# A four-layer block for four sequences: two elements' ternary layers cut in two, their rounded rows held in WKV's buffers

## The chip, the cores and the metric

The kernel runs on one core of a Trainium2 chip. A core has a matrix engine (TensorE, "PE" in the profile, with "PEld" for its weight loads), a vector engine (VectorE, "DVE"), a scalar engine (ScalarE, "ACT"), a general engine (GpSimd, "POOL") and SyncE ("SP"), whose queue issues the DMAs here. Each engine works through its own queue in order; semaphores tie the queues to each other. The metric is the device time of one execution in microseconds (us). Lower is better.

## What is computed

Four sequences ("elements", b = 0 to 3) of 512 rows and 512 columns go through four layers, each added to x with a gate:

```python
x = x + tanh(g_xattn[0]) * wkv(layernorm(x), context)
x = x + tanh(g_ffn[0])   * bit_ffn(layernorm(x))      # 512 -> 2048 -> 512, 1-bit weights
x = x + tanh(g_xattn[1]) * attention(layernorm(x), context)   # 16 heads, int8 rounding
x = x + tanh(g_ffn[1])   * ternary(layernorm(x), gamma, W)

def ternary(x, gamma, W):
    xn = x * rsqrt(mean(x * x) + 1e-6) * gamma
    a = 127 / (max(abs(xn), row) + 1e-5)
    x_q = clip(round(xn * a), -128, 127) / a
    w = 1 / (mean(abs(W)) + 1e-5)
    w_q = clip(round(W * w), -1, 1) / w
    return x_q @ w_q.T
```

`bit_ffn` rounds its input, and the product of its two halves, to int8 with one scale for each 64 columns, and its weights to their sign. The elements don't depend on each other. The change concerns the last layer, the ternary one.

## The kernel before

Rows are worked on in tiles of 128 (NT = 4 tiles an element), all in float32 or in pairs of halves, and each element's x stays on the chip (`xb`). The four elements form a pipeline. While the FFN of element b runs on PE, the attention of element b - 1 is threaded between its matmuls, and the WKV layer of element b + 1 as well. The FFN of an element takes 16 units (NT row tiles x NF = 4 column blocks, `ff_hp` and `ff_acc` in the profile); the attention takes 64 score blocks (`s_ps`, `at_nm`, `at_P`, `pt_ps`, `at_PT`, `o_ps`).

The order of this is written out by hand. Every layer is a generator that yields after each step; `line(gen, (start, end, steps), ...)` gives its steps places on an axis on which 1 is one element's FFN and 1/SLOTS (SLOTS = 17) is one unit; and `run` always advances the generator whose next step has the smallest place. PE's instructions come out in this order. On the other engines a scheduler orders them by when their inputs are expected; each engine's queue is then fixed. A line marked `aside` is put near the end of the unit in which its place lies.

On that axis the FFN of element b runs from b to b + 16/17. The attention of element b has its 72 unit steps from `start` = b + 1 + 4.95/17 to `end` = `start` + 18/17, so it reaches a little into the next element's FFN; the attention of the last element has no FFN beside it. The ternary layer of element b follows its attention, `late_by` behind `end`: 8 units later for b = 0, 9 for b = 1. So the ternary layer of b = 0 lies beside the fourth element's FFN's start (rounding and products within some 700 to 782 us of the trace) and that of b = 1 behind the last FFN (some 892 to 953 us). That of b = 2 lies beside the last element's attention (some 987 to 1022), and that of b = 3 ends the kernel.

A row tile of the ternary layer goes like this (`ternary`, lines 1130 to 1175). For b = 0 and 1, POOL centres and scales the rows (`centred_aside`, L219) and multiplies by gamma (L1148) into `tf_xn`; for b = 2 and 3, DVE does both in one instruction (L1141). DVE takes the largest absolute value (`absmax`, L222) and derives the factors in `tf_s` with small operations (L1152, L1153, L1159, L1160). ACT rounds (`rounded`, L231). Then come the products: four PE transposes into a bank `qr_ps` (L165, called in `transposed_rows`), an ACT copy that takes the rounding constant away (L238, `tf_xT`), four PE matmuls into `f_ps` (L162), DVE's addition to x (L1173), and the output's DMA on SP (L1174). `in_steps(chains, 1)` runs the four tiles one step apart.

Where the buffers lie: `tf_xn` of b = 0 comes from a ring of ROWS = 3 rows, `at_row`, which the attention's own rows `at_xn` use too; for b = 1 to 3 it comes from a ring of three in the FFN's pool. `tf_s` has a ring of four. `qr_ps`, `f_ps` and the attention's `pt_ps`, `ot_ps` and `o_ps` share the three PSUM banks with the tag `m`; the FFN's `ff_hp` and the attention's scores `s_ps` use the three with the tag `hp`. The WKV layer keeps its work in a pool of its own, among it `wk_k` and `wk_e`, each [128, 4, 512] float32, last used by the WKV of the last element.

Other names in the text: the FFN's quantiser takes group maxima (`qg_s`, L222, L676), rounds (`qg_i`, L680), casts on ACT into the single buffer `qg_b` (L684) and scales back on POOL (`ff_xn` or `ff_z`, L685); `ff_z` is formed by ACT L745, DVE L746 and L750; `tp_ps` are the FFN's transposes; L773 adds the FFN's result to x. In the attention, `at_nm` is the score maximum (DVE L948), `at_P` the exponential (ACT L950), `at_PT` the copy of the transposed weights (DVE L968 or ACT L970), L1000 and L1036 the scaling of results, and L1037 the addition to x on POOL. Its queries are rounded and projected (`at_xn`, `at_s`, `q_ps`, `at_half`), written to DRAM by the DMA `qD` and fetched again in the layout of the scores by `at_qR`, both on SP's queue. The layer norm takes its statistics on DVE (L191, L194, L200, L204) and its square root on POOL (L180, L207), giving `ln_r` and `ln_m`.

Of the kernel before, what the change touches and what calls it, by code (L numbers as in the profile page):

```python
# [10 lines left out]
F32 = mybir.dt.float32  # L11
F32R = mybir.dt.float32r
BF16 = mybir.dt.bfloat16
# [8 lines left out]
P = 128  # L22
# [8 lines left out]
def kernel(  # L31
# [37 lines left out]
    NB, T, D = x.shape  # L69
    FF = w1.shape[0]  # L70
    NT, NC, NF = T // P, D // P, FF // D
# [4 lines left out]
    ROWS = 3  # L76
# [4 lines left out]
    sm = ctx.enter_context(tc.tile_pool(name="small", bufs=4))  # L81
    ring = ctx.enter_context(tc.tile_pool(name="ring", bufs=5))
    ff = ctx.enter_context(tc.tile_pool(name="ffn", bufs=2))
    wk = ctx.enter_context(tc.tile_pool(name="wkv", bufs=1))
# [46 lines left out]
    def bank(name, dtype=F32):  # L131

        return psum_tile(name, "m", dtype)
# [22 lines left out]
    def next_turn():  # L156

        if "last" in turn:
            turn["ahead"] = turn["last"]

    def matmul(*args, **kwargs):
        return in_turn(nc.tensor.matmul(*args, **kwargs))  # L162
# [54 lines left out]
    def centred_aside(dst, xb, r, t):  # L217

        nc.gpsimd.tensor_scalar(dst, xb[:, t, :], r[t][0], r[t][1], ALU.mult, ALU.add)  # L219

    def absmax(dst, src):
        nc.vector.tensor_reduce(dst, src, AX.X, ALU.max, apply_absolute_value=True)  # L222
# [6 lines left out]
    def rounded(src, r):  # L229

        nc.scalar.activation(src, src, AF.Identity, bias=magic[:, 0:1], scale=r)  # L231

    def transposed_rows(dst, src):

        pt = bank("qr_ps")
        for c in range(NC):
            transpose(pt[:, c * P : (c + 1) * P], src[:, c * P : (c + 1) * P], ident)
        nc.scalar.activation(dst, blocks(pt), AF.Identity, bias=magic[:, 1:2])  # L238

    def in_steps(chains, delay):  # L240


        ahead = []
        for j, chain in enumerate(chains):
            lag = delay * j if isinstance(delay, int) else delay[j]
            ahead += [(k + lag, -j, chain) for k in range(10)]
        for _, group in groupby(sorted(ahead, key=lambda a: a[:2]), key=lambda a: a[0]):
            went = False
            for _, _, chain in group:
                went = next(chain, None) is not None or went  # L250
                next_turn()
            if went:
                yield
# [22 lines left out]
    class Weights:  # L276
# [130 lines left out]
        def ternary(self):  # L407
            wn = self.raw.pop("f")
            mf = self.mean_abs(self.fsum, D * D)
            nc.vector.tensor_scalar(mf, mf, 1e-5, None, ALU.add)  # L410
            nc.vector.tensor_scalar(
                coef[:, 3:4], mf, gates[:, 3:4], 1.0 / 127.0, ALU.mult, ALU.mult
            )
            rf = cp.tile([P, 1], F32, name="rf")
            nc.vector.reciprocal(rf, mf)
            wi = self.pool.tile([P, NC, D], BF16, name="wi", tag="sg", bufs=2)
            self.ints["f"] = wi
            yield
            for j in range(NC):
                rounded(wn[:, j, :], rf)  # L420
                nc.vector.tensor_scalar(
                    wn[:, j, :], wn[:, j, :], MAGIC + 1.0, MAGIC - 1.0, ALU.min, ALU.max
                )
                nc.scalar.activation(
                    wi[:, j, :], wn[:, j, :], AF.Identity, bias=magic[:, 1:2]
                )
                yield
# [412 lines left out]
    def attention_layer(b, xb, pool, tiles=range(NT)):  # L840
# [209 lines left out]
        def end(ts):  # L1050

            yield from together([project_out(t) for t in ts])
            means, scale = statistics(b, xb, ts)
            yield from together([ternary(b, xb, pool, t, means, scale) for t in ts])
# [57 lines left out]
    def statistics(b, xb, tiles):  # L1112
# [13 lines left out]
        at = {t: slice(i, i + 1) for i, t in enumerate(tiles)}  # L1126
        return {t: m[:, at[t]] for t in tiles}, {t: y[:, at[t]] for t in tiles}

    def ternary(b, xb, pool, t, r, scale=None):


        last = b > NB - 3
        behind_ffn = b > NB - 4
        if behind_ffn:

            xn = ff.tile([P, D], F32, name="tf_xn", tag="ff_a", bufs=3)
        else:
            xn = pool.tile([P, D], F32, name="tf_xn", tag="at_row", bufs=ROWS)
        s = sm.tile([P, 3], F32, name="tf_s", tag="tf_s")
        if last:  # L1140
            nc.vector.scalar_tensor_tensor(  # L1141
                xn, xb[:, t, :], r[t], gamma_b, ALU.add, ALU.mult
            )
            absmax(s[:, 0:1], xn)
            nc.vector.tensor_scalar(s[:, 0:1], s[:, 0:1], scale[t], 1e-5, ALU.mult, ALU.add)
        else:
            centred_aside(xn, xb, r, t)
            nc.gpsimd.tensor_tensor(xn, xn, gamma_b, ALU.mult)  # L1148
            yield True
            yield True  # L1150
            absmax(s[:, 0:1], xn)
            nc.vector.tensor_scalar(s[:, 0:1], s[:, 0:1], 1e-5, None, ALU.add)  # L1152
        nc.vector.reciprocal(s[:, 1:2], s[:, 0:1])  # L1153
        if last:
            nc.vector.tensor_scalar(
                s[:, 1:2], s[:, 1:2], scale[t], 127.0, ALU.mult, ALU.mult
            )
        else:
            nc.vector.tensor_scalar(s[:, 1:2], s[:, 1:2], 127.0, None, ALU.mult)  # L1159
        nc.vector.tensor_tensor(s[:, 2:3], s[:, 0:1], coef[:, 3:4], ALU.mult)  # L1160
        rounded(xn, s[:, 1:2])
        yield True
        if behind_ffn:
            xT = ring.tile([P, NC, P], BF16, name="tf_xT", tag="w")
        else:
            xT = pool.tile([P, NC, P], BF16, name="tf_xT", tag="at_oqT")
        transposed_rows(xT, xn)
        yield True
        fp = bank("f_ps")
        for c in range(NC):  # L1170
            matmul(fp, lhsT=xT[:, c, :], rhs=wfT[:, c, :], start=(c == 0), stop=(c == NC - 1))
        xt = xb[:, t, :]
        nc.vector.scalar_tensor_tensor(xt, fp, s[:, 2:3], xt, ALU.mult, ALU.add)  # L1173
        nc.sync.dma_start(out=out[b, t * P : (t + 1) * P, :], in_=xt)  # L1174
        yield True
# [17 lines left out]
    def late(make):  # L1193
        yield from make()

    def place(line):

        k = line["step"]
        for start, end, steps in line["parts"]:
            if k < steps:  # L1200
                at = start + (end - start) * k / steps

                return (math.floor(at * SLOTS) + 0.8) / SLOTS if line["aside"] else at
            k -= steps
        return end

    def run(until):
        while lines:
            now = min(lines, key=place)
            if place(now) > until:  # L1210
                return
            try:
                next(now["gen"])
                now["step"] += 1
                next_turn()
            except StopIteration:
                lines.remove(now)
# [3 lines left out]
    SLOTS = NT * NF + 1  # L1221

    def line(gen, *parts, aside=False):
        lines.append({"gen": gen, "parts": parts, "step": 0, "aside": aside})

    xs = {}
# [122 lines left out]
    for b in range(NB):  # L1349
        if b:  # L1350
            early = (0.99, 1.0, 4) if b == 1 else (b - 0.19, b - 0.1, 3), (b - 0.08, b, 1)
            line(
                late(lambda b=b: ffn_layer(xs[b])),
                *((early[0],) if b == 1 else early),
                (b, b + 16 / SLOTS, 64),
                (b + 16 / SLOTS, b + 17.75 / SLOTS, 7),
            )
        start = b + 1 + 4.95 / SLOTS
        end = start + 18 / SLOTS
        line(  # L1360
            late(lambda b=b: attention_layer(b, xs[b], at)),
            (b + 1.0 if b == 0 else b + 0.7, b + 1.03 if b == 0 else b + 0.9, 5),
            (b + 1 + 1.7 / SLOTS, b + 1 + 3.7 / SLOTS, 5),
            (b + 1 + 3.75 / SLOTS, b + 1 + 4.35 / SLOTS, 2),
            (start, end, 72),
            (end, end + 2.4 / SLOTS, 6)
            if b != NB - 2
            else (end - 0.15 / SLOTS, end + 4.65 / SLOTS, 6),
            (end + 2.4 / SLOTS, end + 3.4 / SLOTS, 4),
        )  # L1370
        if b < NB - 1:
            late_by = (8 / SLOTS, 9 / SLOTS, 0.0)[b]
            line(
                late(lambda b=b: ternary_layer(b, xs[b], at)),
                (end + 3 / SLOTS + late_by, end + 8 / SLOTS + late_by, 8)
                if b < NB - 2
                else (end + 4.85 / SLOTS, end + 11.85 / SLOTS, 7),
                aside=b < NB - 2,
            )
    run(NB + 9)  # L1380


# [43 lines left out]
```

## Time and profile before

| | us |
|---|---|
| median of 3 runs (lowest to highest) | 1079.84 (1078.74 to 1081.25) |
| the profiled execution, its whole time | 1080.4 |
| its span, from the first instruction to the last | 1078.6 |
| mean granted PE clock | 0.967 |

The profile page covers one execution. Its first part gives each engine's busy time and its share of the span; its second part cuts the span in 40 slices of 27 us and gives the busy share of each slice in tenths. A stretch view gives the same for windows of one's choice. A timeline row has the start in us, the duration (of the whole group where an instruction comes several times in a row, "x2"), the engine, the source line, the operation, out<-in, and in brackets the idle time of the engine just before it and the instruction that ended it. Ends of PE matmuls are modelled, and neighbouring ones overlap. Two other rows of the page, the engines behind PE, in tenths of a slice:

```profile
DVE  5976547747876799987669799977687858799876
POOL 3831114413423244632215526333121303200000
```

The vector engine is busiest, beside PE, from about 860 us on; POOL has next to nothing to do in the last 130 us.

The costliest waits of the whole run, engine by engine (in total, times, longest), are few and short on PE, and longer on the engines that serve it:

```profile
POOL ff_z L685 <- ACT qg_b L684: 287.2, 50, 12.6
ACT at_PT L970 <- PE pt_ps L165: 70.8, 99, 2.2
ACT at_P L950 <- DVE at_nm L948: 38.1, 57, 4.2
```

### The profile page before, as it was taken

What the parts mean: (1) busy time and instruction counts of PE and PEld (TensorE: products, weight loads), DVE (VectorE), ACT (ScalarE), POOL (GpSimd) and SP (SyncE); (2) the same over time, 40 slices, a digit from 0 to 9 for tenths busy, and PEclk for the clock granted to TensorE, in tenths of its full rate; (3) what the DMA queues carried; (4) which work ended last, traced back from release to release, by engine and by line L of the source; (5) the groups of instructions that cost most, each with busy time, mean ns of one, the idle gap of its engine ahead of it and who ended that gap; (6) DMA issues with size and microseconds to landing.
All of it is one profiled execution on the core that took longest, in us unless ns stands there. A gap on an engine that the chain in (4) does not pass through costs nothing.

```text
span 1078.6 us, 17948 instructions
## 1 busy us (share of the span) xinstructions
PE 935.4 (87%) x6353; PEld 675.0 (63%) x6380; DVE 836.0 (78%) x1610; ACT 724.6 (67%) x1480; POOL 321.6 (30%) x328
## 2 busy tenths in 40 slices
PE   3879998998888888889998798999999998888875
PEld 2335565565656666767776476777677777655652
DVE  5976547747876799987669799977687858799876
ACT  6656756476555677667778677777676767777763
POOL 3831114413423244632215526333121303200000
PEclk8889999999999999999999799999999999999998
DMA  8188945365445673744665528445665662254311
GB/s 292 39 257 323 322 172 214 115 225 187 156 137 149 235 242 120 256 133 138 235 196 195 176 92 261 138 165 182 229 232 179 209 218 61 87 158 121 111 39 40
DMA packets 85672, 189.67 MB, mean 176 GB/s; under 512 B 12240, under 2 KB 36816, under 8 KB 74576
## 3 DMA queue, kind: packets, MB, share of 16 engines
q1 hardware_dynamic: 85584, 188.53, 53.2%
q8 instruction: 51, 0.84, 0.3%
q14 instruction: 37, 0.30, 0.1%
HBM read 148.65 MB, written 39.85 MB: 175 GB/s over the span
## 4 chain that ended last, share of the span: by engine, by line
PE 45%; DVE 26%; ACT 13%; issue 5%; DMA 5%; POOL 5%; SPq 1%; ACTq 0%; POOLq 0%; DVEq 0%
PE ff_hp L162 14%; PE pt_ps L165 7%; PE ff_acc L162 5%; PE o_ps L162 4%; ACT at_P L950 3%; PE s_ps L162 3%; DVE at_nm L948 3%; DVE wk_q L640 3%; PE v_ps L162 3%; PE k_ps L162 2%; ACT at_PT L970 2%; DVE wk_p L634 2%; DVE ff_z L750 1%; DVE qg_i L680 1%; PE tp_ps L165 1%
## 5 line engine op out<-in xcount | busy, mean ns | idle before, releaser
L162 PE MATMUL ff_hp<-wT,xp 128*128 128x512 f32 x1024 | 270.8, 406 | 7.6 <-DVE ff_z L746 4.6
L162 PEld LDWEIGHTS ff_hp<-wT,xp 128*128 128x128 f32 x1024 | 192.1, 192 | 53.9 <-DVE ff_z L746 5.7
L950 ACT ACTIVATE at_P<-s_ps,at_nm 128x512 f32<-128x512 f32 x256 | 174.9, 689 | 40.2 <-DVE at_nm L948 38.1
L948 DVE TENSOR_REDUCE at_nm<-s_ps 128x1 f32<-128x512 f32 x256 | 166.3, 676 | 28.8 <-PE s_ps L162 28.3
L970 ACT COPY at_PT<-pt_ps 128x512 f32<-128x512 f32 x214 | 125.9, 590 | 71.7 <-PE pt_ps L165 70.8
L685 POOL TENSOR_TENSOR ff_z<-qg_b,qg_s 128x512 f32<-128x512 bf16 x64 | 72.3, 1130 | 321.4 <-ACT qg_b L684 287.2
L165 PE MATMUL pt_ps<-ident,at_P 128*128 128x128 f32 x1024 | 155.1, 280 | 8.5 <-ACT at_PT L970 4.6
L165 PEld LDWEIGHTS pt_ps<-ident,at_P 128*128 128x128 f32 x1024 | 118.2, 142 | 45.5 <-ACT at_PT L970 11.7
L162 PE MATMUL ff_acc<-wT,hr 128*128 128x512 f32 x512 | 136.7, 407 | 7.4 <-ACT hr L696 3.8
L162 PE MATMUL s_ps<-at_kR,at_qR 128*128 128x512 f32 x256 | 102.5, 460 | 23.1 <-ACT at_P L950 17.6
L162 PEld LDWEIGHTS ff_acc<-wT,hr 128*128 128x128 f32 x512 | 92.1, 189 | 28.8 <-DVE hr L697 5.9
L162 PE MATMUL o_ps<-at_PT,at_V 128*32 128x128 f32 x2048 | 74.9, 278 | 4.5 <-ACT at_PT L970 2.7
L162 PEld LDWEIGHTS o_ps<-at_PT,at_V 128*32 128x32 f32 x2048 | 54.6, 110 | 28.2 <-issue 9.1
L745 ACT ACTIVATE ff_z<-ff_hp,coef 128x512 f32<-128x512 f32 x64 | 44.1, 689 | 40.7 <-PE ff_hp L162 38.4
L746 DVE SCALAR_TENSOR_TENSOR ff_z<-ff_z,ff_hp 128x512 f32<-128x512 f32 x64 | 43.4, 678 | 36.1 <-ACT ff_z L745 35.8
L750 DVE SCALAR_TENSOR_TENSOR ff_z<-ff_hp,coef,ff_z 128x512 f32<-128x512 f32 x64 | 47.7, 746 | 28.6 <-PE ff_hp L162 28.4
L684 ACT CAST qg_b<-qg_i 128x512 bf16<-128x512 int8 x80 | 49.3, 616 | 26.6 <-DVE qg_i L680 18.8
L162 PEld LDWEIGHTS s_ps<-at_kR,at_qR 128*128 128x128 f32 x256 | 43.2, 192 | 36.0 <-ACT at_P L950 25.4
L162 PE MATMUL v_ps<-wkvT,cT 128*128 128x512 f32 x128 | 60.4, 618 | 5.5 <-DVE wT L303 2.3
L162 PE MATMUL k_ps<-cT,wkvT 128*128 128x512 f32 x128 | 60.9, 627 | 2.3 <-ACT wk_k L584 1.0
L640 DVE RECIPROCAL wk_q<-wk_q 128x256 f32<-128x256 f32 x32 | 54.5, 1722 | 2.9 <-POOL wk_q L635 1.5
L950 ACT ACTIVATION_READ_ACCUMULATOR at_P<-s_ps,at_nm 128x1 f32 x256 | 51.8, 202 | 0.0
(180 smaller groups left out, 1663.9 us busy)
## 6 DMA issues: line engine op xcount, KB each, us to landing
wT<-wD SPq DMA_DIRECT2D x72, 1024.0 KB, 5.6
wn<-in_L_ffn_w_dram SPq DMA_DIRECT2D x18, 1024.0 KB, 6.3
at_kR<-kD SPq DMA_DIRECT2D x128, 128.0 KB, 4.6
at_qR<-qD SPq DMA_DIRECT2D x256, 64.0 KB, 2.5
wD<-wT SPq DMA_DIRECT2D x12, 1024.0 KB, 4.2
kD<-k_half SPq DMA_DIRECT2D x16, 512.0 KB, 2.8
qD<-at_half SPq DMA_DIRECT2D x32, 256.0 KB, 2.1
cn<-in_ctx_dram SPq DMA_DIRECT2D x8, 512.0 KB, 6.4
```

Of the source, the lines that this page charges most:

```text
L162: return in_turn(nc.tensor.matmul(*args, **kwargs))
L165: return in_turn(nc.tensor.transpose(*args))
L634: nc.vector.tensor_tensor_scan(p[:, 1:], A2, E2, 0.0, ALU.mult, ALU.add)
L640: nc.vector.reciprocal(half, half)
L684: nc.scalar.copy(qb, qi)
L685: nc.gpsimd.tensor_tensor(grouped(src), grouped(qb), s.unsqueeze(2).to_broadcast([P, NG, GS]), ALU.mult)
L745: nc.scalar.activation(z, hp, AF.Tanh, scale=coef[:, 0:1])
L746: nc.vector.scalar_tensor_tensor(z, z, 1.0, hp, ALU.add, ALU.mult)
L750: nc.vector.scalar_tensor_tensor(z, hp, coef[:, 1:2], z, ALU.mult, ALU.mult)
L948: nc.vector.tensor_reduce(nm, sp, AX.X, ALU.max, negate=True)
L950: nc.scalar.activation(lanes[k, i, t], sp, AF.Exp, bias=nm, accum_out=sums[k][:, t, i : i + 1],)
L970: made[k] = nc.scalar.copy(dst, blocks(pt))
```

## The change

For b = 0 and b = 1 the ternary layer is cut in two behind the rounding.

The first part, `ternary`, ends with `rounded` for these two elements, in 6 steps instead of 8. For b = 0 it starts where it did. For b = 1 it starts nine units earlier (`late_by` is 0), at place 3.53, some 816 us on the trace of before, beside the last element's FFN. The rounded rows of all four tiles stay on the chip: those of b = 0 in the buffer with WKV's tag `wk_k`, those of b = 1 in `wk_e`, and the factors of each element in a tile of its own, `tf_s0` and `tf_s1`. So `tf_xn` of b = 0 no longer uses the ring `at_row`.

The second part, `ternary_products`, has the transposes, the products, the addition and the output's DMA. For b = 0 and 1 a new line, `ternary_ends`, runs it for four tiles in 5 steps over 3.2 units, from place 4 + 0.6/17 for b = 0 and from 4 + 3.8/17 for b = 1: behind the last element's FFN, while the third element's attention ends and the last one's is prepared. The transposed rows `tf_xT` of b = 0 come from the ring `w`, as those of the others did. For b = 2 and 3 the two parts follow each other as before.

The lines move: L1148 becomes L1160, the small operations L1164, L1165, L1171 and L1172, the addition L1186 and the output's DMA L1187.

```diff
+    held = {}
+
+    def held_rows(b, t):
+        if b not in held:
+            rows = wk.tile([P, NT, D], F32, name="tf_xn", tag=("wk_k", "wk_e")[b])
+            factors = sm.tile([P, NT, 3], F32, name="tf_s", tag=f"tf_s{b}", bufs=1)
+            held[b] = rows, factors
+        rows, factors = held[b]
+        return rows[:, t, :], factors[:, t, :]
+
+    def ternary_ends(b, xb):
+        yield from in_steps([ternary_products(b, xb, t, *held_rows(b, t)) for t in range(NT)], 1)
+
     def ternary(b, xb, pool, t, r, scale=None):
         last = b > NB - 3
-        behind_ffn = b > NB - 4
-        if behind_ffn:
+        if last:
             xn = ff.tile([P, D], F32, name="tf_xn", tag="ff_a", bufs=3)
+            s = sm.tile([P, 3], F32, name="tf_s", tag="tf_s")
         else:
-            xn = pool.tile([P, D], F32, name="tf_xn", tag="at_row", bufs=ROWS)
-        s = sm.tile([P, 3], F32, name="tf_s", tag="tf_s")
+            xn, s = held_rows(b, t)
...
         rounded(xn, s[:, 1:2])
         yield True
-        if behind_ffn:
-            xT = ring.tile([P, NC, P], BF16, name="tf_xT", tag="w")
-        else:
-            xT = pool.tile([P, NC, P], BF16, name="tf_xT", tag="at_oqT")
+        if last:
+            yield from ternary_products(b, xb, t, xn, s)
+
+    def ternary_products(b, xb, t, xn, s):
+        xT = ring.tile([P, NC, P], BF16, name="tf_xT", tag="w")
         transposed_rows(xT, xn)
...
         if b < NB - 1:
-            late_by = (8 / SLOTS, 9 / SLOTS, 0.0)[b]
+            late_by = 8 / SLOTS if b == 0 else 0.0
             line(
                 late(lambda b=b: ternary_layer(b, xs[b], at)),
-                (end + 3 / SLOTS + late_by, end + 8 / SLOTS + late_by, 8)
+                (end + 3 / SLOTS + late_by, end + 6.75 / SLOTS + late_by, 6)
                 if b < NB - 2
                 else (end + 4.85 / SLOTS, end + 11.85 / SLOTS, 7),
                 aside=b < NB - 2,
             )
+            if b < NB - 2:
+                at_end = NB + (0.6 + 3.2 * b) / SLOTS
+                line(
+                    late(lambda b=b: ternary_ends(b, xs[b])),
+                    (at_end, at_end + 3.2 / SLOTS, 5),
+                )
```

## The prediction

> **What bounds the kernel now.** I read the page's busy shares and slices first, then the busy time by stretch around the places that the change touches, then the timeline of single engines there.
>
> ```profile
> PE 935.4 (87%) x6353; PEld 675.0 (63%) x6380; DVE 836.0 (78%) x1610; ACT 724.6 (67%) x1480; POOL 321.6 (30%) x328
> ...
> PE   3879998998888888889998798999999998888875
> ```
>
> TensorE (PE) leads with 87%, and the slices show that it isn't even: 90% and more from 674 to 890 us, 80% behind it. The stretches (window, length, then busy us and instructions of PE, PEld, DVE, ACT, POOL; then granted PE clock, DMA share, GB/s):
>
> ```profile
> 738.00:782.00 44.00, 42.34 (x310) 31.29 (x312) 32.18 (x70) 30.54 (x63) 12.21 (x12) 1.00 0.54 183
> 782.00:900.00 118.00, 116.40 (x891) 92.22 (x894) 87.60 (x195) 85.92 (x191) 25.98 (x27) 1.00 0.62 197
> 900.00:912.00 12.00, 9.84 (x108) 7.55 (x109) 11.44 (x27) 9.37 (x24) 4.98 (x5) 1.00 0.26 67
> 912.00:950.00 38.00, 31.65 (x310) 23.15 (x310) 28.61 (x67) 26.08 (x59) 6.89 (x8) 0.96 0.35 106
> 950.00:1050.00 100.00, 84.26 (x914) 60.87 (x922) 86.90 (x188) 75.29 (x193) 1.46 (x1) 1.00 0.35 101
> ```
>
> From 738 to 900 (the FFN of the third and fourth element beside attention) PE is busy 96% and 99%: PE work put in lengthens the run by itself, and work taken out shortens it. From 900 on PE is at 82 to 84% and the vector engine (DVE) at 75 to 95%: what counts is which engine answers the next score or transpose, and PE has holes. The change takes PE work out of the first kind of stretch and puts it into the second; it also moves rounding the other way.
>
> **Prices.** The groups of the ternary tiles (duration min/median/max in ns, first and last start):
>
> ```profile
> L162 PE MATMUL f_ps<-wfT,tf_xT x56: 376/379/634, 752.0 to 1074.0; 128*128 128x512 bf16 x56
> L165 PE MATMUL qr_ps<-ident,tf_xn x64: 272/273/474, 740.3 to 1072.2; 128*128 128x128 f32 x64
> L219 POOL TENSOR_SCALAR tf_xn<-xb,ln_r x8: 766/768/772, 703.1 to 926.5; 128x512 f32<-128x512 f32 x8
> L1148 POOL TENSOR_TENSOR tf_xn<-tf_xn,gamma_b x8: 1260/1282/1745, 704.5 to 927.3; 128x512 f32<-128x512 f32 x8
> ```
>
> On PE the starts count, since matmuls overlap: in the timeline the four transposes of a tile begin at 769.11 and its products at 769.60, the next work at 770.47. So 0.49 + 0.87 = 1.36 us a tile; 1.3 is taken, 5.2 for four. Products also cost 0.69 of ScalarE (ACT, L238) and 0.745 of DVE (L1173) a tile; rounding costs 0.77 + 1.28 of GpSimd (POOL), 0.675 (L222) and some 0.6 of small ones on DVE, 0.82 of ACT (L231).
>
> **A. The first element's rounding becomes one POOL run: +3.7.** Before, a ring of three rows let only two tiles be rounded ahead; the third waited until the first had been transposed (POOL rows at 741.07 and 752.30). Now all four have rows of their own, and the changed program's order has POOL do L219 twice, L1148 twice, and both again, before ff_xn and ff_z. Before, two tiles stood there (the timeline of POOL, then ACT, then PE):
>
> ```profile
> 703.06 1.52 POOL L219 TENSOR_SCALAR tf_xn<-xb,ln_r 128x512 f32<-128x512 f32 x2
> 704.55 3.00 POOL L1148 TENSOR_TENSOR tf_xn<-tf_xn,gamma_b 128x512 f32<-128x512 f32 x2
> ...
> 707.51 1.49 POOL L685 TENSOR_TENSOR ff_xn<-qg_b,qg_s 128x512 f32<-128x512 bf16 x1
> ...
> 709.03 0.62 ACT L684 CAST qg_b<-qg_i 128x512 bf16<-128x512 int8 x1 [0.61 <-POOL ff_xn L685]
> ...
> 709.56 0.68 ACT L950 ACTIVATE at_P<-s_ps,at_nm 128x512 f32<-128x512 f32 x1
> ...
> 710.38 2.12 PE L162 MATMUL ff_hp<-wT,xp 128*128 128x512 f32 x8 [0.53 <-ACT at_P L950]
> ```
>
> Two tiles took 707.51 - 703.06 = 4.45; by means 2 x (0.77 + 1.28) = 4.1. Two more put ff_xn's start at about 711.7. qg_b has one buffer, so the ACT cast at 709.03 waits for ff_xn, behind it the exp at 709.56, and PE's ff_hp waits for the score bank that this exp empties. The row has already 0.53 of PE idle there, so nothing is left as cover. Of the 4.1 to 4.45 I take 3.7, since work ready on the other engines shortens what follows; range 2.5 to 4.5.
>
> **B. The first element's products leave 738–782: -3.8.** 5.2 us of PE go, and with them the POOL waits (6.7 us at 752.30, behind which at_xn of the third element stood). Of the four tiles the first is hidden at 740 (the next transpose waits for an ACT copy anyway); 751.54–752.97, 767.07–770.47 and 780.62–781.48 are 1.4, 3.4 and 0.9 of bare PE time. Against that, the first scores of the third element (781.83) wait for a chain that shortens less: q product 765.14, qD issue 771.26, qR issue 774.89, landing 779 to 781. Where PE arrives 4 us sooner, this DMA can be what is late next. Range -6.5 to -2. The four output DMAs leave SP's queue there (it stood behind them) and join the tail's.
>
> **C. The second element's rounding goes into 816–832: +1.2.** POOL has a hole there (idle from 818.95 to 831.11), and four tiles of 2.05 to 2.25 (8.2 to 9) fill it. In the changed order DVE's L222 of the first tile stands right behind L746 of 820.34, and needs more first: from L1037's end at 818.95, 1.16 of layer norm on DVE (L191 0.68, L194, L200 and L204 0.16 each), 1.2 on POOL (L180, L207), two L219 and one L1148, so 824.1. Behind it stand L773 (822.59), two score maxima (823.26) and L750 (825.33). The maxima come some 2.3 late, and the exps, next scores and ff_hp (827.14) about 1.2 of that, the rest is slack. Range 0 to 2.5.
>
> **D. The same rounding leaves 892–912: -1.5.** There it hurts today:
>
> ```profile
> 900.85 1.16 DVE L676 TENSOR_SCALAR qg_s<-qg_s 128x8 f32<-128x8 f32 x1
> ...
> 904.83 1.02 DVE L1160 TENSOR_TENSOR tf_s<-tf_s,coef 128x1 f32<-128x1 f32 x1
> ...
> 907.44 0.63 PE L165 MATMUL tp_ps<-ident,ff_z 128*128 128x128 f32 x4 [1.30 <-ACT at_PT L970]
> ```
>
> The same two small operations take 0.14 to 0.16 elsewhere (L676 at 827.39, L1160 at 911.90), so DVE loses 1.9 beside POOL's row operations. ACT's L231 at 906.01 then waits for the factors, the copy at_PT behind it is late, and PE idles 1.30. I take 1.5 of these as returned; range 0.5 to 2.5.
>
> **E. The first element's products enter the tail (917–930), the second element's stay: +2.8.** 5.2 us of PE at the tail's ratio of elapsed to busy time (38.00/31.65 = 1.20) would be 6.2. One hole is there to be filled: PE idles 2.82 before the transposes of at_xn at 928.88. DVE loses three tiles of rounding (1.3 each, and a wait of 1.62 for L1148 at 928.63) and gains four L1173 (3.0), so it is no worse. Against the relief, the changed DVE order puts L222 of at_xn right behind L194, where it waits for POOL (1.2 of L180 and L207, 0.77 of L219: 2.0); 1.0 of it is taken, since at_xn itself comes earlier by it. 6.2 - 2.8 - 1.6 (the DVE wait gone) + 1.0 = 2.8. The lower end is 0: all of it in PE's holes. The upper: the products and transposes share three `m` banks with the four pt, the o and the ot of an attention unit, 6 allocations in a unit of about 4.94 us (916.93 to 921.87); two more at the same turnover are 4.94 x 2/6 = 1.65 a tile, 6.6 in all. A look at the stretch with the third element's tiles: six units with one whole tile each (o_ps from 985.33 to 1022.36) took 37.03, against three plain ones at 5.57 (1022.36 to 1039.08), so 0.60 a tile, rounding included, or 2.4 for four. That row is nearest, and the 2.8 stays.
>
> The held rows lie in WKV's buffers `wk_k` and `wk_e`. Their last reader before is a transpose at 682.1, and the first new write comes at 703: no wait, cost 0.
>
> **Sum.** 3.7 - 3.8 + 1.2 - 1.5 + 2.8 = +2.4. The durations belong to the profiled execution of 1080.4 (span 1078.6 and 1.8 around it), which thus becomes 1082.8; the median of the runs, 1079.84, lies 0.56 lower, so the forecast is 1082.2.
>
> [...]
>
> **Rivals.** First, on the other side: the tail takes the products in its holes. For it: PE is 16% idle from 912 to 950, DVE and ACT become lighter there, and the tiles come without the chain that now makes DVE wait for POOL. Then E is 0, and, if the third element's queries also come early (at_xn no longer stands behind the tf_xn that waited 6.70), B is its full -6.5, and D -2.0: 3.7 - 6.5 + 1.2 - 2.0 + 0 = -3.6, 1076.2. It decides once B passes 6.2 with E at 0. Against it: the chain of DMAs named in B.
>
> Second, the three banks: each product tile pushes a pt transpose back by 1.65, E is 6.6: 1079.84 + 6.2 = 1086.0. For it: PE waits in the tail mostly for the copies that empty banks (DVE L968, ACT L970), and both engines stay above 68% busy. Against it: the stretch of the third element showed 0.60.
>
> Third, the POOL run costs nothing at the end: the stall at 710 only delays work that waits at 781 for the query DMA anyway. A falls to 0.5, or B to nothing with A at 0: about 0.5 - 3.8 + 1.2 - 1.5 + 2.8 = -0.8, 1079.0, no change. Against it: between 712 and 781 stand 70 us in which PE is the bound.
>
> Fourth, the split doesn't act: the held buffers still waited for, or the products placed otherwise than in program order. The changed program, where the products stand behind the last FFN, speaks against both; if it were so, the tail lengthens by the bare 5.2 of PE and nothing is returned, 1079.84 + 5.2 = 1085.0.
>
> **How the numbers follow.** Forecast 0.35, first rival 0.29, second 0.19, third 0.15, fourth 0.02. The likeliest case is 1082.2, its own range 1079.5 to 1085 from C and E moving by half their bounds. To hold 8 in 10 the range has to reach the first rival's value and the second's with a little beyond: 1075.2 to 1086.8. No change is within 0.2% (2.16 us, about what a measurement of this kernel can tell), 1077.7 to 1082.0. Faster: 0.26 of the first rival, 0.03 of the third, 0.02 of the forecast, 0.31. Slower: 0.25 of the forecast, 0.19, 0.02 of the third and 0.02, 0.48. The rest, 0.21, is no change.
>
> **What will show it.** A: POOL's ff_xn at about 711.7 with the L684 cast idle before it for some 4 us, and PE idle before ff_hp for over 3. B: the distance from there to the first scores of the third element (71.5 now, 710.38 to 781.83) shorter by 4, and PE or s_ps waiting for the at_qR DMA there. C: DVE's L222 at about 821 waiting some 3 us for POOL. D: L676 back to 0.16 at about 900 and no PE wait of 1.30. E: from the last ff_acc (about 902.6) to the first o_ps of the last element longer by 3 than now. The prediction is wrong if PE's wait at 710 stays under 1 us (A), or if the tail from the last ff_acc to the end is no longer than now (E).

## The result and the profile after

| | before | after |
|---|---|---|
| median of 14 runs each (lowest to highest), us | 1080.82 (1076.08 to 1082.93) | 1086.32 (1082.04 to 1089.10) |
| span of the profiled execution, us | 1078.6 | 1084.6 |

The ratio after to before is 1.0053, with a 95% interval of 1.0041 to 1.0064: the change makes the kernel slower by 0.53%, some 5.7 us. The forecast had the sign, and the range (1075.2 to 1086.8) held the time by 0.5, but it said +2.4. (The 14 runs of the kernel before have a median 1.0 above that of the three that stand ahead of the prediction.)

The page of the kernel after, busy shares, and the clock's row of the slices:

```profile
PE 942.7 (87%) x6380; PEld 677.7 (62%) x6380; DVE 830.3 (77%) x1610; ACT 724.5 (67%) x1480; POOL 321.0 (30%) x328
...
PEclk8889999999999999999999799989999999999997
```

The shares tell nothing: 87% again, and PE's busy times can't be set against each other, since the trace of before has 27 matmul records fewer (x6353 against x6380) of the same number. But the clock row has an 8 in the slice from 705 us, where it was 9. The stretches show it (same columns as in the prediction):

```profile
709.00:714.00 5.00, 0.54 (x2) 0.19 (x1) 2.79 (x6) 0.97 (x2) 4.27 (x5) 0.97 0.39 93
714.00:717.00 3.00, 2.62 (x6) 2.15 (x7) 0.00 (x0) 2.15 (x7) 0.76 (x1) 0.50 1.02 429
717.00:720.00 3.00, 3.00 (x12) 2.29 (x11) 1.80 (x5) 0.68 (x2) 0.00 (x0) 0.50 0.48 202
```

Between 709 and 714 PE does almost nothing while POOL is at 4.27 of 5, and in the six microseconds behind it the granted clock is 0.50. The stretches 900 to 912 and 912 to 950 are fuller on PE, as they were to be: 11.90 and 34.20 us busy instead of 9.84 and 31.65.

To see where the time goes, one can follow a landmark that both kernels have. The first matmul of each `ff_acc` group is one: there are twenty from 694 us to the end of the last FFN, in the same order in both timelines. Their start after, minus their start before, in us (start before in the left column):

| landmark | after - before | what lies between it and the one above |
|---|---|---|
| 706.19 | +0.07 | |
| 717.79 | +6.45 | the first element's rounding (A) |
| 758.29 | +4.02 | |
| 785.32 | -1.16 | its products gone (B) |
| 820.48 | -0.30 | |
| 830.49 | +3.85 | the second element's rounding (C) |
| 851.55 | +5.13 | |
| 902.61 | +5.19 | |
| 911.55 | +4.09 | the same rounding gone from here (D) |
| end of the span, 1078.6 | +6.0 | the first element's products (E) |

So A is +6.4 (forecast +3.7), B from 717.79 to 820.48 is -6.8 (-3.8), C is +5.4 (+1.2), D is -1.0 (-1.5) and E +1.9 (+2.8).

**A, in the timeline after** (POOL, then ACT, then PE):

```profile
703.13 1.52 POOL L219 TENSOR_SCALAR tf_xn<-xb,ln_r 128x512 f32<-128x512 f32 x2
704.62 2.98 POOL L1160 TENSOR_TENSOR tf_xn<-tf_xn,gamma_b 128x512 f32<-128x512 f32 x2
707.59 1.95 POOL L219 TENSOR_SCALAR tf_xn<-xb,ln_r 128x512 f32<-128x512 f32 x2
709.51 2.48 POOL L1160 TENSOR_TENSOR tf_xn<-tf_xn,gamma_b 128x512 f32<-128x512 f32 x2
711.96 1.04 POOL L685 TENSOR_TENSOR ff_xn<-qg_b,qg_s 128x512 f32<-128x512 bf16 x1
...
713.03 0.62 ACT L684 CAST qg_b<-qg_i 128x512 bf16<-128x512 int8 x1 [4.54 <-POOL ff_xn L685]
713.55 0.68 ACT L950 ACTIVATE at_P<-s_ps,at_nm 128x512 f32<-128x512 f32 x1
...
714.38 3.78 PE L162 MATMUL ff_hp<-wT,xp 128*128 128x512 f32 x8 [4.48 <-ACT at_P L950]
```

The chain is the forecast one: ff_xn at 711.96 (forecast 711.7), the cast 4.54 late, the exp behind it, and ff_hp, which PE reaches after 4.48 of idle time. What the forecast lacks is in the last row: the eight matmuls of ff_hp take 3.78 instead of 2.12.

**C, in the timeline after** (POOL, DVE, ACT, PE):

```profile
823.45 2.52 POOL L1160 TENSOR_TENSOR tf_xn<-tf_xn,gamma_b 128x512 f32<-128x512 f32 x2
...
824.77 0.69 DVE L222 TENSOR_REDUCE tf_s<-tf_xn 128x1 f32<-128x512 f32 x1 [3.62 <-POOL tf_xn L1160]
825.37 0.74 DVE L773 SCALAR_TENSOR_TENSOR xb<-ff_acc,coef,xb 128x512 f32<-128x512 f32 x1
826.03 1.28 DVE L948 TENSOR_REDUCE at_nm<-s_ps 128x1 f32<-128x512 f32 x2
...
826.74 0.69 ACT L950 ACTIVATE at_P<-s_ps,at_nm 128x512 f32<-128x512 f32 x1 [3.42 <-DVE at_nm L948]
...
827.58 0.50 PE L162 MATMUL s_ps<-at_kR,at_qR 128*128 128x512 f32 x1 [1.59 <-ACT at_P L950]
828.72 0.66 PE L165 MATMUL pt_ps<-ident,at_P 128*128 128x128 f32 x4 [0.64 <-ACT at_PT L970]
...
829.45 3.31 PE L162 MATMUL ff_hp<-wT,xp 128*128 128x512 f32 x8
```

DVE stands 3.62 at a maximum that needs POOL, the maxima of the scores behind it are 2.8 late (826.03 against 823.26), and PE waits 1.59 for their exps and then 0.64 for the copy at_PT; ff_hp takes 3.31 instead of 1.99 (before, at 827.14).

### The profile page after: what moved, and what is told of

Its sections match the earlier page's. It is cut to its first block, busy times and chain, and to the rows that moved or that the text cites. A ratio compares the mean times of both kernels' runs of the same rounds, so it can differ in the third digit from the quotient of the medians.

```text
span 1084.6 us, 17972 instructions
## 1 busy us (share of the span) xinstructions
PE 942.7 (87%) x6380; PEld 677.7 (62%) x6380; DVE 830.3 (77%) x1610; ACT 724.5 (67%) x1480; POOL 321.0 (30%) x328
## 4 chain that ended last, share of the span: by engine, by line
PE 45%; DVE 26%; ACT 13%; POOL 6%; issue 5%; DMA 5%; SPq 1%; ACTq 0%; DVEq 0%; POOLq 0%
PE ff_hp L162 14%; PE pt_ps L165 7%; PE ff_acc L162 5%; PE o_ps L162 4%; PE s_ps L162 3%; DVE wk_q L640 3%; PE v_ps L162 3%; ACT at_P L950 3%; DVE at_nm L948 3%; PE k_ps L162 2%; ACT at_PT L970 2%; DVE wk_p L634 2%; DVE ff_z L750 1%; PE qr_ps L165 1%; PE tp_ps L165 1%
## 5 line engine op out<-in xcount | busy, mean ns | idle before, releaser
L162 PE MATMUL ff_hp<-wT,xp 128*128 128x512 f32 x1024 | 275.8, 412 | 11.7 <-ACT at_P L950 6.4
L162 PEld LDWEIGHTS ff_hp<-wT,xp 128*128 128x128 f32 x1024 | 194.9, 195 | 59.0 <-ACT at_P L950 8.1
L685 POOL TENSOR_TENSOR ff_z<-qg_b,qg_s 128x512 f32<-128x512 bf16 x64 | 72.8, 1138 | 335.3 <-ACT qg_b L684 315.3
```

The lines of the kernel that those rows point to most:

```text
L685: nc.gpsimd.tensor_tensor(grouped(src), grouped(qb), s.unsqueeze(2).to_broadcast([P, NG, GS]), ALU.mult)
```

## The experiments

All are set against the changed kernel unless it is said otherwise. Each time stands beside runs of the kernel before on the same chip, and a ratio is to those. The landmarks give a second reading, from one profiled execution each, in the terms A to E (us; a landmark's difference to before less that of the one above; the starts of ff_acc at 706.19, 717.79, 820.48, 851.55, 911.55 and the span's end):

| kernel | A | B | C | D | E | ratio to before (95%) |
|---|---|---|---|---|---|---|
| after | 6.4 | -6.8 | 5.4 | -1.0 | 1.9 | 1.0053 (1.0041 to 1.0064) |
| two_tiles | 0.0 | -5.4 | 4.1 | -1.1 | 2.7 | 1.0014 (0.9999 to 1.0030) |
| two_buffers | 0.8 | -6.8 | 5.6 | -1.1 | 0.8 | 1.0002 (0.9990 to 1.0014) |
| late_maxima | 6.0 | -6.9 | 1.0 | -1.2 | 0.4 | 1.0013 (0.9997 to 1.0029) |
| second_only | 0.0 | 0.5 | 5.8 | -1.1 | -1.3 | 1.0051 (1.0031 to 1.0071) |
| first_only | 6.4 | -7.3 | 0.0 | 0.0 | 1.8 | 1.0019 (1.0003 to 1.0036) |
| three_tiles | 3.7 | -6.8 | 5.7 | -1.2 | 0.9 | one run |
| both_buffers | 0.8 | -6.8 | 0.7 | -1.3 | 0.2 | 0.9968 (0.9951 to 0.9985) |
| both_pinned | 0.0 | -5.4 | 1.0 | -1.1 | 1.3 | 0.9972 (0.9956 to 0.9988) |
| before_two_buffers | -0.8 | 0.0 | 0.0 | 0.1 | -0.5 | 1.0003 (0.9988 to 1.0019) |
| no_first_products | 0.8 | -6.7 | 0.7 | -1.2 | -2.4 | 0.9955 (0.9940 to 0.9970) |

A to D repeat to some tenths wherever their cause is the same, but for C in two_tiles (4.1 instead of 5.4 to 5.8), which the part on C below takes up. E moves by over 2 us, 0.2 to 2.7, between the seven kernels with one and the same tail (the first four rows, three_tiles and the two with both repairs), so it is known less well. Two of those traces differ in the clock: in after it falls to 0.50 behind two waits of the tail (952.06 and 1057.32; 0.98 from 950 to 1050), and the eight matmuls behind the second, `p_ps` at 1058.76, take 3.43; in both_buffers it is 1.00 from 912 to 1050, and behind the wait of 1.30 at 1046.63, the same as that at 1057.32, four of `p_ps` take 1.04. Their E is 1.9 and 0.2.

**two_tiles.** Is A the long run on POOL?

```diff
-        yield from in_steps([ternary(...) for t in range(NT)], 1)
+        lags = (0, 1, 4, 6) if b == 0 else 1
+        yield from in_steps([ternary(...) for t in range(NT)], lags)
...
-            centred_aside(xn, xb, r, t)
+            row = centred_aside(xn, xb, r, t)
+            if b == 0 and t > 1:
+                tc.keep_in_program_order(row)
...
-                (end + 3 / SLOTS + late_by, end + 6.75 / SLOTS + late_by, 6)
+                (end + 3 / SLOTS + late_by, end + (6.75, 8.625)[b == 0] / SLOTS + late_by, (6, 9)[b == 0])
```

> The changed kernel, but the third and fourth tile of the first element are centred and multiplied on POOL some units later (their POOL operations pinned to a later place), so that only two tiles stand before ff_xn, as in the kernel before. Theory (the run of four on POOL holds ff_xn, the cast behind it and PE's ff_hp, 4.0 us of idle time and some 2.4 us of halved clock behind it): ff_xn starts at 707.5, no PE wait over 1 us at 710, the first fourteen units lose the 6.4, and the time is 1086.3 - 6.4 = 1080, a little over if the later tiles now hit something (up to +2). Rival (the stall only delays work that waits later anyway, and the loss lies in the tail's banks): 1086 as it was.

Measured: 1081.65 (before 1080.14), A 0.0. The two tiles that come later take some 1.4 of B back. The rival, that the stall costs nothing at the end, is refuted: the intervals of two_tiles (up to 1.0030) and of the changed kernel (from 1.0041) don't meet.

**two_buffers.** Which link passes the lateness on?

```diff
-        qb = ff.tile([P, D], BF16, name="qg_b", tag="qg_b", bufs=1)
+        qb = ff.tile([P, D], BF16, name="qg_b", tag="qg_b", bufs=2)
```

> The changed kernel with two buffers for qg_b instead of one, nothing else; the run of four tiles on POOL stays. Theory (the single buffer passes POOL's lateness through ACT's cast and the exp behind it to ff_hp): the cast and the exp come on time, ff_hp starts near 710.4, and what is left is the transposes of ff_xn waiting till some 713.3, about 1 us; no halved clock at 714. A falls from 6.4 to 1 or 1.5, the time to some 1081, and ff_xn itself still starts at 712. [...]

Measured: 1080.27 (before 1080.14), A 0.8. The order of instructions is the same on every engine. Its timeline, PE, POOL and ACT:

```profile
710.15 2.05 PE L162 MATMUL ff_hp<-wT,xp 128*128 128x512 f32 x8
...
712.42 1.03 POOL L685 TENSOR_TENSOR ff_xn<-qg_b,qg_s 128x512 f32<-128x512 bf16 x1
...
708.73 0.62 ACT L684 CAST qg_b<-qg_i 128x512 bf16<-128x512 int8 x1
...
713.51 0.66 PE L165 MATMUL tp_ps<-ident,ff_xn 128*128 128x128 f32 x4 [1.30 <-POOL ff_xn L685]
```

ff_xn is as late as in the changed kernel (this execution stands 0.4 later as a whole), but the cast no longer waits for it, and ff_hp runs on time and at full speed (2.05, and 2.12 before). PE waits 1.30 where it really needs ff_xn. So the run on POOL is the cause, and the single buffer with ACT's queue behind it the link that made 6.4 of it; POOL being busy beside DVE is not.

**three_tiles.** How does A grow with the run, and when does the clock fall? The edit is that of two_tiles with `t > 2`, lags (0, 1, 2, 5) and 8 steps.

> The changed kernel with three tiles of the first element on POOL before ff_xn, the fourth pinned later; to see how the wait grows with the run and whether the clock falls. Theory for the wait: a tile costs POOL 2.05, so ff_xn starts at 709.8 and PE's ff_hp waits 4.48 - 2.05 = 2.4. For the clock there are two readings: it falls only behind a longer hole, then the fourteen-unit table shows a loss of 1.9 here; or any hole of over 2 us halves it for some microseconds, then ff_hp takes over 3 us again and the loss is 3.5 to 4.5.

Measured: 1081.41 in its one run, A 3.7. From its timeline and from its stretches:

```profile
711.22 2.89 PE L162 MATMUL ff_hp<-wT,xp 128*128 128x512 f32 x8 [2.64 <-ACT at_P L950]
```

```profile
712.00:715.00 3.00, 3.00 (x12) 2.42 (x11) 0.85 (x4) 0.99 (x4) 0.00 (x0) 0.56 0.93 382
```

The wait is 2.64 (2.4 expected), and the clock falls behind it, to a mean of 0.56 from 712 to 715. So the loss is that of the second reading. With the four points: idle 0.53 (before), 1.30 (two_buffers), 2.64 and 4.48 go with 0, 0.8, 3.7 and 6.4 of loss. Beyond the idle time itself (less the 0.53 that was there) that is 0, 0, 1.6 and 2.4. For any hole of over 2 us the second reading does not hold: behind PE's wait of 3.02 at 919.46 in no_first_products four transposes take 0.66, the time of full speed (1.11 at a clock of 0.50 in the kernel before, at 928.88). The last section has what goes with a fall.

**late_maxima.** Is C the wait in DVE's queue?

```diff
     def absmax(dst, src):
-        nc.vector.tensor_reduce(...)
+        return nc.vector.tensor_reduce(...)
...
-            absmax(s[:, 0:1], xn)
+            largest = absmax(s[:, 0:1], xn)
+            if b == 1:
+                tc.keep_in_program_order(largest)
```

> The changed kernel, but the four DVE maxima (L222) of the second element's tf_xn are pinned to their later place in program order; POOL's order is the same. Theory (DVE waits in its queue 3.6 us for POOL's gamma product, and behind it stand the FFN's addition, the score maxima and L750): no DVE wait over 1 us at 821, PE no longer idles at 826 to 829 and keeps its full clock at 830 to 832, C falls from 5.4 to about 1, the time to 1086.3 - 4.4 = 1082. [...]

Measured: 1081.17 (before 1080.14), C 1.0. POOL's order is unchanged and its four tiles still run beside PE's FFN, so it was the place in DVE's queue that cost, not POOL's work. Nor was it ACT's roundings: they move later here too, but in the changed kernel the first of them starts at 835.19, behind the stall. The 1.0 that is left comes between the landmarks 830.49 and 851.55. From its timeline, DVE and POOL:

```profile
821.29 0.75 DVE L773 SCALAR_TENSOR_TENSOR xb<-ff_acc,coef,xb 128x512 f32<-128x512 f32 x1 [1.16 <-PE ff_acc L162]
...
826.08 2.97 DVE L676 TENSOR_SCALAR qg_s<-qg_s 128x8 f32<-128x8 f32 x1
...
824.96 1.54 POOL L219 TENSOR_SCALAR tf_xn<-xb,ln_r 128x512 f32<-128x512 f32 x2
...
826.45 2.58 POOL L1160 TENSOR_TENSOR tf_xn<-tf_xn,gamma_b 128x512 f32<-128x512 f32 x2
```

L773 now waits for PE alone. The second row is for the last section.

**second_only and first_only.** Do the halves add up? In second_only the first element's ternary layer is that of before (ring `at_row`, `at_oqT`, products at its old place); in first_only the second element's is (ring `ff_a`, `late_by` 9/17, products right behind the rounding). The lines that decide, with comments added here:

```diff
-            late_by = 8 / SLOTS if b == 0 else 0.0
+            late_by = (8 / SLOTS, 9 / SLOTS, 0.0)[b]        # first_only
...
-            if b < NB - 2:
+            if b == 0:                                      # first_only; second_only: b == 1
                 at_end = NB + (0.6 + 3.2 * b) / SLOTS
```

> The kernel before with the second element's part of the change alone (rounding at 816 to 832, products behind the last FFN); the first element's ternary layer as before, products at 740 to 781. Theory (the parts add up): C +5.4 and D -1.1, that is 1080.8 + 4.3 = 1085; no stall at 710, PE idle and halved clock at 826 to 832 as in the changed kernel. Rival (C exists only since the first element's products left PE's queue and everything else came earlier): about 1080, no change.

> The kernel before with the first element's part of the change alone (four tiles on POOL at 703, products behind the last FFN); the second element's ternary layer as before, whole behind the last FFN. Theory (the parts add up: A +6.4, B -6.8, E +1.9 or more, since the second element's rounding now stays in the tail beside the products): 1080 + 1.5 to 4 = 1081.5 to 1084, PE idle 4.5 with halved clock behind it at 710 to 720, no stall at 826. Rival (the two halves of the change only hurt together): 1080, no change.

Measured: second_only 1085.41 (before 1080.14), first_only 1082.07 (before 1080.37). Each shows its own terms and none of the other's; 0.51% and 0.19% make 0.70% where the whole change has 0.53%, within their intervals. The larger loss is the second half, which moves rounding; its products stay in the tail.

**both_buffers, both_pinned, before_two_buffers.** What is the change worth without its two stalls? The edits are those of two_buffers with late_maxima, of two_tiles with late_maxima, and of two_buffers alone on the kernel before.

> The changed kernel with both repairs: two buffers for qg_b, and the second element's DVE maxima pinned to their later place. Theory (A and C are separate and add up; what is left of the change is the shorter PE-bound stretch, B and D, against the tail): A 0.8 as with the two buffers alone, C 1.1 as with the late maxima alone, so the time is 1086.3 - 5.6 - 4.3 = 1076.4, below the kernel before (1080.1 to 1080.8) by 4. Rival (either repair only lets the work run into the next wait, which sets the end): 1080 to 1081, as each repair alone.

> The changed kernel with only two tiles on POOL before ff_xn (the other two pinned later), and the second element's maxima pinned later. Theory: A 0 and C 1.1, so 1086.3 - 6.4 - 4.3 = 1075.6; the two later tiles of the first element cost up to 1.5 where they now come, as they did alone (B was 6.3 instead of 7.6 there). Rival as for the two buffers: 1080 to 1081.

> The kernel before with two buffers for qg_b, nothing else. Theory (the second buffer helps only where POOL is late; before, the cast waited 0.61 for it at 709 and PE 0.53): at most 0.6 faster, 1079.5 to 1080.5, no difference that can be told. Rival (the second buffer is a gain by itself, all over the FFN, and hides what the change costs): 1076 or less.

Measured: 1075.24, 1075.81 and 1079.80, beside 1079.66 before. By the ratios the repairs add up to within a microsecond, and with both the kernel is faster than before by 0.3% (both intervals lie below 1). The second buffer by itself gives nothing that shows in the time; at its place the landmark comes 0.8 earlier.

**no_first_products.** What do the four tiles cost in the tail? This kernel is both_buffers and leaves out the first element's products:

```diff
+        if b == 0:
+            yield True
+            nc.sync.dma_start(out=out[b, t * P : (t + 1) * P, :], in_=xb[:, t, :])
+            yield True
+            return
         transposed_rows(xT, xn)
```

> The kernel with both repairs by buffers and maxima, without the first element's transposes, products and additions: its rows are written out as they are before the ternary product. It measures what these four tiles cost where they now stand. Theory of the sum (some fill PE's holes, E 1.9 to 2.8): 1075.2 - 2 to 3 = 1072.5. Rivals: 1075 if they lie wholly in holes, 1069 if each pushes an attention unit back by its share of the banks (6.6).

Measured: 1075.14 (before 1080.37). By the landmarks the tail is 2.5 shorter than in both_buffers (E -2.4 against 0.2), as the theory has it, but that is one execution, the fastest of the twelve (1069.40). The time itself is the one that the rival in holes gave, 1075; set against the kernel before, the two ratios, 0.9955 and 0.9968, lie 1.4 us apart and their intervals overlap. So 6.6 is excluded, and whether the four tiles cost 2.5 or next to nothing isn't settled.

## Why the prediction was right, and where it was wrong

**What bounds the kernel: right.** PE work taken out of the stretch up to 900 shortened the run by what it was and more, and the same work cost less in the tail, E 0.2 to 2.7.

**A, the run on POOL: place and chain right, size wrong.** The forecast had the idle time, 3.7, against 4.48 - 0.53 = 3.95 measured. The missing 2.4 is PE's halved clock behind the hole (0.50 from 714 to 720), a term that the sum put at nothing, and the upper bound of 4.5, made from POOL's durations alone, could not hold it. The trace of before had it to be read: behind its own hole of 2.82 at 928.88, which the prediction names under E, the clock is 0.50 (from 928.70 to 932.12), and four transposes take 1.11 instead of 0.66:

```profile
925.41 0.66 PE L165 MATMUL qr_ps<-ident,tf_xn 128*128 128x128 f32 x4 [0.21 <-DVE at_PT L968]
928.88 1.11 PE L165 MATMUL qr_ps<-ident,at_xn 128*128 128x128 f32 x4 [2.82 <-ACT at_xn L231]
```

two_tiles, three_tiles and two_buffers show the cause and the link.

**B, the products leaving: wrong by 3.** The step that failed is "this DMA can be what is late next". In the changed kernel the scores of the third element follow without a wait for `at_qR` (a wait would stand in brackets):

```profile
780.66 0.71 PE L162 MATMUL s_ps<-at_kR,at_qR 128*128 128x512 f32 x2
```

The query chain came earlier with the rest (its issue of `at_qR` at 773.06 instead of 774.89), it seems since at_xn no longer stood behind the POOL operation that waited 6.70. So nothing was given back there, and -6.8 exceeds even the lower bound of -6.5; at 785.32 it is -7.6, and 0.9 of that is lost again by 820.48, for a part to the second element's rounding (0.5 in second_only). PE's busy time between the landmarks 726.71 and 820.48 falls by 6.1 (91.19 to 85.06), more than the 5.2 counted from starts, though the trace shows only 27 of the 32 matmuls as gone. This is read from the traces; no experiment put the query chain alone to the test, though every kernel with the products moved and POOL's order kept shows the same 6.7 to 7.3.

**C, the second element's rounding: the mechanism right, the price wrong by 4.** The maximum was expected at 824.1 and came at 824.77, and the right instructions stood behind it. The step that failed is "some 1.2 of that, the rest is slack". There was no slack on PE in a stretch that is 99% busy: the delay of 2.8 at the score maxima became 1.59 and 0.64 of PE idle, another 1.3 of slowed ff_hp, and 1.3 more up to 851. late_maxima removes all but 1.0 of it. The slowed part is the halved clock again (0.50 from 829.79 to 833.20), and it is not in every execution: two_tiles has the same waits, 1.57 and 0.64, but its ff_hp takes 1.99, and its C is 4.1.

```profile
823.60 0.50 PE L162 MATMUL s_ps<-at_kR,at_qR 128*128 128x512 f32 x1 [1.57 <-ACT at_P L950]
...
825.47 1.99 PE L162 MATMUL ff_hp<-wT,xp 128*128 128x512 f32 x8
```

**D: right** (-1.0 for -1.5). DVE's small operations are fast again (L676 takes 0.16 at 906.04, instead of 1.16 at 900.85), and the wait of 1.30 before the transposes is gone.

**E: within its range, and no better known than that** (1.9 for 2.8). The table's other values for this tail, 0.2 to 2.7, say how well one profile knows it. One part was foreseen elsewhere: what B feared at 781 happens in the tail, where PE waits 1.65 for `at_qR` at 952.06.

**The rivals.** The second came nearest in time, 1086.0, and is wrong: the banks of the tail would have put 6.6 into E. The first (the tail takes the products in its holes) was near the truth for B, and for E as far as that is known; it lost since A and C are dearer than both cases thought. That the repaired kernels land near its 1076.2, at 1075.2 and 1075.8, doesn't confirm it, since its sum holds 3.7 for A where they have 0.8 and 0. The third is refuted by two_tiles: without the stall the end comes some 4.2 earlier (1.0014 for 1.0053). The fourth is refuted by B: work did leave that stretch. The sum was mis-sized by +2.7 in A, -3.0 in B and +4.2 in C. That errors of both signs kept the total within the range is luck.

## What to carry to other kernels

Work moved onto an engine with time to spare is paid where something stands behind it: read the queue of that engine, and the single buffers between it and the engine that bounds the kernel, before its busy share. Where the bounding engine is at 99%, price every late releaser in full and allow for the slower clock behind a hole (here 0.50 for 3.4 to 6.8 us behind some of them), rather than discount for slack that the share rules out. And a change that loses may hold a gain: one more buffer and four instructions pinned later turned +0.5% into -0.3%.

## What the runs showed of the hardware

**A hole in PE's work can cost twice.** The clock was 0.50 for six microseconds behind the hole of 4.48, 0.56 over three behind that of 2.64, and in second_only 0.51 from 832 to 834 behind waits of 1.59 and 0.64 in a row:

```profile
832.00:834.00 2.00, 2.00 (x7) 1.52 (x6) 1.80 (x5) 0.98 (x3) 0.00 (x0) 0.51 0.00 0
```

The hole's length alone doesn't decide. The clock stayed at 1.00 behind 1.30 in two_buffers (713.51), and even behind 3.02 in no_first_products (919.46) four transposes took 0.66, the time of full speed; it fell behind 1.65 in the kernel after (952.06). What goes with a fall can be read from the traces of before and after, by the clocks of short stretches; no experiment was made for it. In the kernel after the three falls between 640 and 1050 begin at 713.73, 829.79 and 952.67: 116.06 and 122.88 apart, 34.0 and 36.0 times 3.413. The clock is back at 1.00 after 6.83, 3.41 and 3.41. In the kernel before there is one fall in that time, at 928.70, for 3.41. With both traces cut into stretches of 3.41 from these falls, PE had been idle in the one before each fall for 3.41, 1.85, 1.92 and 2.76. In no other such stretch at full clock between 640 and 1050 was it idle for more than 1.52. So in these two traces a hole that left PE idle for 1.85 or more of one such stretch cost some 1.7 beyond its length, or twice that (an estimate: half of 3.41 and of 6.83, less what falls into the hole). Why the same two waits cost nothing more in two_tiles (ff_hp 1.99 behind them) was not shown.

**A small DVE operation can last as long as several of POOL's.** In late_maxima the L676 on 128x8 numbers, with a median of 0.16 in the kernel before, took 2.97, from 826.08 to 829.05; the two L1160 beside it ended at 829.03. So it lasted over the end of one POOL operation (L219, at 826.50) and the two that followed. In the kernel before, the L676 of 1.16 ended at 902.01 and the L1160 of 1.02 at 905.85, the POOL operations beside them at 901.99 (L1148) and 905.84 (L685): one each. The cause was not put to a test. In late_maxima it cost nothing that the landmarks show at 830 (the difference to before is the same at 820.48 and 830.49, -1.3), as PE had its work.
